# Attention scores turned round: keys on the partitions, the greatest score through two small turnings, sums through a product with ones

## The chip, the cores and the metric

The kernel runs on one NeuronCore of a Trainium2 chip. The core has five engines that run side by side, each working through its own list of instructions in order. TensorE (PE in the profile; its weight loads are listed as PEld) multiplies matrices and writes its results into PSUM, a small memory of eight banks of 512 fp32 columns on each of 128 partitions. VectorE (DVE), ScalarE (ACT) and GpSimd (POOL) work elementwise on SBUF, the main on-chip memory; of the three only DVE and ACT reach PSUM in this kernel. SyncE (SP) issues DMAs. The metric is the device time of one execution in microseconds (us), as the median of several runs.

## What is computed

Four layers, each added to a residual stream x of 16 batches of 100 tokens and 512 channels: cross attention with 16 heads, a mixture of eight experts, cross attention with 8 heads, and an FFN with quantized weights. The change touches the two attentions alone. All is fp32.

```python
q = (query @ Wq + bq).reshape(B, Nq, H, D).transpose(0, 2, 1, 3)
k = (key_value @ Wk + bk).reshape(B, Nkv, H, D).transpose(0, 2, 1, 3)
v = (key_value @ Wv + bv).reshape(B, Nkv, H, D).transpose(0, 2, 1, 3)
attn = jnp.einsum('bhqd,bhkd->bhqk', q, k) * scale
attn = jnp.clip(attn, -CLAMP, CLAMP)
attn = jax.nn.softmax(attn, axis=-1)
...
x = jnp.einsum('bhqk,bhkd->bqhd', attn, v).reshape(B, Nq, Cq)
return x @ Wo + bo
...
x = x + jnp.tanh(g_xattn[0]) * _L0_xattn_ref(_layernorm(x, axis=-1), ctx_768, ...)
x = x + jnp.tanh(g_ffn[0]) * _L0_ffn_ref(_layernorm(x, axis=-1), ...)
x = x + jnp.tanh(g_xattn[1]) * _L1_xattn_ref(_layernorm(x, axis=-1), ctx_768, ...)
x = x + jnp.tanh(g_ffn[1]) * _L1_ffn_ref(_layernorm(x, axis=-1), ...)
```

A batch has 100 queries (T) and 722 keys (S) whose input has 384 channels. In layer 0 a head has D = 32 channels, so G = 4 heads fill a block of 128 partitions; in layer 1 D = 64 and G = 2. The second attention has no clamp and no biases bq, bk, bv.

## The kernel before

**Steps.** `Attention.run` (L500) goes over 64 steps (b, m): 16 batches, and for each the KC = 4 blocks m of 128 channels. One step handles the G heads of its block. For a step the kernel computes scores, takes exp, turns the exps round and multiplies them with the values.

**Scores** (`scores`, L356). The queries of a head, a slice `qT` of D partitions and 100 columns, are the stationary operand; the keys `kT` stream past in two halves of 361 columns (SH). The result `ps_s` has the queries on the partitions and the keys along the columns. The G heads lie on different partitions of the array and write to different banks. DVE copies them out with the sign turned, and the same instruction gives the least of the negated scores in each row (L389 for layer 1, L402 for layer 0): with queries on the partitions the greatest score of a query lies within one row. In layer 0 the two halves are parts 0 and 1, recorded at different places of a step, and L412 joins their extremes. The array `extremes` keeps them for a later test (`unusual`, L1116) of whether the clamp could have mattered.

**Exp** (`softmax`, L417). ACT computes exp for each head with the negated greatest score as the bias of each row, into one of six (layer 1: four) buffers `pr`, and the same instruction adds up the row (`sums`).

**Turning** (`turn`, L430). The product with the values needs the keys on the partitions. So each head's exps are turned on PE in six pieces of up to 128 keys (L444), 24 pieces a step in layer 0 and 12 in layer 1, and ACT and DVE in turns copy the results from PSUM (L457, L459) to `pT`. The reciprocals of the sums, spread over D columns (L439), are turned likewise (L452), one piece a step.

**Weighted sum** (`attend`, L462). For six pieces of keys and G heads, PE multiplies the values (stationary) with `pT` (100 columns) into `ps_pv`. DVE multiplies the result with the turned reciprocal (L475) and writes it to `tT`.

**What fills the steps.** `run` also deals out units of other work: the keys (`keys`, L208) and values (`values`, L230) of the following batches, 14 units a batch, and the units in `extra`: queries (L332), the inputs of queries (L312), output projections (L482), and in layer 0 the routing work of the experts that follow. A step in layer 0 is recorded in this order: part 0 of the next step's scores, weighted sum of the step before, two fifths of the units, turnings of the first pair of heads, a fifth of the units, part 1 of the next scores, turnings of the second pair, the rest of the units, exp of the next step. In layer 1 all scores are computed together and there is one pair.

**What sets the order.** PE runs its instructions in the order in which they are recorded (`manual_schedule(engines={PE})`); for the other engines a scheduler chooses. Buffers come from pools, and an allocation waits until the last use of the buffer that it reuses is over. PSUM's eight banks are split into `ps_s` (two buffers of two banks, for scores) and `ps_m` (four buffers of one bank, for everything else: `ps_k`, `ps_v`, `ps_q`, `ps_t`, `ps_pv`, `ps_y`, `ps_tr`).

Of the kernel before, what the change touches and what calls it, by code (L numbers as in the profile page):

```python
# [8 lines left out]
F32 = mybir.dt.float32  # L9
# [17 lines left out]
SL = S - (NS - 1) * P  # L27
GB = 4
# [113 lines left out]
class Attention:  # L142
# [43 lines left out]
    def first_keys(self):  # L186
# [3 lines left out]
        two = [self.ps_s.tile([P, 2, 512], F32, tag="s", name="ps_k2") for _ in range(2)]  # L190
        banks = [t[:, c, :SH] for t in two for c in range(2)]
# [63 lines left out]
    def open(self, ctx):  # L255
# [3 lines left out]
        self.p3, self.p4 = pool("3", 3), pool("4", 4)  # L259
        self.ps_s, self.ps_m = pool("s", 2, space=PSUM), pool("m", 4, space=PSUM)  # L260
# [3 lines left out]
        for n in ("bq", "bv"):  # L264
# [6 lines left out]
        self.probs = [  # L271
            self.pw.tile([T, NS * P], F32, name=f"pr{i}_{name}") for i in range(6 if self.G == 4 else 4)
        ]
        for t in self.probs:
            nc.gpsimd.memset(t[:, S:], 0.0)
        self.qT, self.nmax, self.sums, self.negated, self.pT = {}, {}, {}, {}, {}
# [79 lines left out]
    def scores(self, b, m, part):  # L356

        nc, D, G = self.net.nc, self.D, self.G
        g, i = divmod(b, GB)
        q = slice(i * T, (i + 1) * T)  # L360
        if m == 0 and part == 0:
            self.nmax[b] = (
                self.p2.tile([T, self.heads], F32, tag="nm", name=f"nm_{self.name}_{b}")
                if self.extremes is None
                else self.extremes[:, b * self.heads : (b + 1) * self.heads]
            )
            self.sums[b] = self.p2.tile(
                [T, self.heads], F32, tag="sums", name=f"sums_{self.name}_{b}"
            )
        if part == 0:  # L370
            self.negated[b, m] = [
                self.p4.tile([T, S], F32, tag="ns", name="ns") for _ in range(G)
            ]
        pss = [self.ps_s.tile([T, 2, 512], F32, tag="s", name="ps_s") for _ in range(2)]

        banks = [(j, part) for j in range(G)] if G == 4 else [(j, c) for j in range(2) for c in range(2)]
        for n in sorted(range(4), key=lambda n: banks[n][1]):
            j, c = banks[n]
            nc.tensor.matmul(  # L379
                pss[n // 2][:, n % 2, :SH],  # L380
                self.qT[g][j * D : (j + 1) * D, m, q],
                self.kT[b, m][j * D : (j + 1) * D, c * SH : (c + 1) * SH],
                start=True,
                stop=True,
            )
        nm = self.nmax[b][:, m * G : (m + 1) * G]
        if G == 2:
            for j in range(2):
                nc.vector.tensor_scalar(  # L389
                    self.negated[b, m][j].rearrange("p (c s) -> p c s", c=2),  # L390
                    pss[j][:, :, :SH],
                    -1.0,
                    BIG,
                    ALU.mult,
                    ALU.min,
                    accum_out=nm[:, j : j + 1],
                )
            return
        if part == 0:
            self.halves = self.p2.tile([T, 2, G], F32, tag="nmh", name="nmh")  # L400
        for j in range(G):
            nc.vector.tensor_scalar(  # L402
                self.negated[b, m][j][:, part * SH : (part + 1) * SH],
                pss[j // 2][:, j % 2, :SH],
                -1.0,
                BIG,
                ALU.mult,
                ALU.min,
                accum_out=self.halves[:, part, j : j + 1],
            )  # L410
        if part == 1:
            nc.vector.tensor_tensor(nm, self.halves[:, 0, :], self.halves[:, 1, :], ALU.min)  # L412

    def prob(self, b, h):
        return self.probs[(b * self.heads + h) % len(self.probs)]

    def softmax(self, b, m):  # L417
        nc, G = self.net.nc, self.G
        for j, ns in enumerate(self.negated.pop((b, m))):
            h = m * G + j  # L420
            nc.scalar.activation(  # L421
                self.prob(b, h)[:, :S],
                ns,
                AF.Exp,
                bias=self.nmax[b][:, h : h + 1],
                scale=-1.0,
                accum_out=self.sums[b][:, h : h + 1],
            )

    def turn(self, b, m, pair):  # L430


        nc, D, G = self.net.nc, self.D, self.G
        last = pair == G // 2 - 1
        t = self.p3.tile([P, 2 * NS + 1, T], F32, tag="pT", name="pT")
        if last:
            rinv = self.p2.tile([T, G, D], F32, tag="rinv", name="rinv")
            sums = self.sums[b][:, m * G : (m + 1) * G]
            nc.vector.reciprocal(rinv, bcast(sums.unsqueeze(2), T, G, D))  # L439
        for q in range(3):  # L440
            ps = self.ps_m.tile([P, 5, T], F32, tag="mm", name="ps_t")
            for i in range(4):
                j, c = divmod(4 * q + i, NS)
                nc.tensor.transpose(  # L444
                    ps[:, i, :],
                    self.prob(b, m * G + 2 * pair + j)[:, c * P : (c + 1) * P],
                    self.net.ident[:T, :T],
                )
            n = 4
            if last and q == 2:  # L450
                n = 5
                nc.tensor.transpose(  # L452
                    ps[:, 4, :], rinv.rearrange("p g d -> p (g d)"), self.net.ident[:T, :T]
                )
            to = t[:, 4 * q : 4 * q + n, :]
            if (m + pair + q) % 2:
                nc.scalar.copy(to, ps[:, :n, :])  # L457
            else:
                nc.vector.tensor_copy(to, ps[:, :n, :])  # L459
        self.pT[b, m, pair] = t  # L460

    def attend(self, b, m):  # L462
        nc, D, G = self.net.nc, self.D, self.G
        ps = self.ps_m.tile([P, T], F32, tag="mm", name="ps_pv")
        for c in range(NS):
            n = P if c < NS - 1 else SL
            for j in range(G):
                nc.tensor.matmul(  # L468
                    ps[j * D : (j + 1) * D, :],
                    self.v[b][:n, c, m * P + j * D : m * P + (j + 1) * D],  # L470
                    self.pT[b, m, j // 2][:n, j % 2 * NS + c, :],
                    start=(c == 0),
                    stop=(c == NS - 1),
                )
        nc.vector.tensor_tensor(  # L475
            self.tT[:, m, b * T : (b + 1) * T],
            ps,
            self.pT[b, m, G // 2 - 1][:, 2 * NS, :],
            ALU.mult,
        )  # L480
# [18 lines left out]

    def run(self, given, after_project=None, more=()):  # L500
# [3 lines left out]
        parts = 2 if self.G == 4 else 1  # L504
# [1096 lines left out]
```

## Time and profile before

Three runs gave 2827.48, 2832.17 and 2833.72 us, a median of 2832.17. The profiled execution took 2827.75 us, its span from first to last instruction 2826.0 us.

| stretch (us from the start) | what runs | length | PE busy | DVE busy | ACT busy | POOL busy |
|---|---|---|---|---|---|---|
| 62 to 936 | layer 0, most of the steps | 874 | 867.8 | 440.8 | 431.2 | 21.9 |
| 936 to 956 | layer 0, its last steps | 20 | 17.4 | 14.5 | 15.2 | 0.8 |
| 1200 to 1640 | experts | 440 | 439.6 | 41.3 | 36.2 | 16.1 |
| 1840 to 2400 | layer 1, most of the steps | 560 | 560.0 | 190.1 | 201.4 | 8.2 |
| 2400 to 2826 | end of layer 1, FFN | 426 | 414.2 | 84.8 | 68.7 | 43.3 |

Views used below. *Sums by stage* give for a stretch its length and the busy time (and count) of PE, PEld, DVE, ACT and POOL, then the clock that PE was granted (1.00 is full), the share of DMA and GB/s. The *timeline* lists instructions in order of time, alike ones that follow each other merged: start, time from the first one's start to the last one's end, engine, line, operation, result and operands, shape, count, and in brackets an idle time before and what ended it. In a matmul's shape 32*100 is the stationary operand (partitions * columns) and 32x361 the streaming one. An ordinary fp32 product appears as two matmul records, a turning as one. Since matmuls overlap, what one costs is the time to the next start, not its own length.

### The profile page before, as it was taken

How to read it: one execution, taken by the hardware profiler on the slowest of the kernel's cores; microseconds unless marked ns; L12 is line 12 of the kernel's file. 1: busy time of each engine (PE TensorE's matmuls, PEld its weight loads, DVE VectorE, ACT ScalarE, POOL GpSimd, SP SyncE). 2: the span in 40 equal slices, each digit the busy share in tenths (PEclk: the TensorE clock that was granted, in tenths of full speed). 3: DMA queues.
4: the chain of work that ended last, by engine and by line, in shares of the span. 5: the costliest groups of instructions: out<-in, count | busy, mean ns of one | idle time of the engine just before them, and what ended most of it. 6: DMA issues, size and time to landing. Idle time of an engine off the chain costs nothing. (4 is left out here: it accounts for less than half of the span.)

```text
span 2826.0 us, 41052 instructions
## 1 busy us (share of the span) xinstructions
PE 2787.1 (99%) x17360; PEld 1732.2 (61%) x17360; DVE 933.4 (33%) x2441; ACT 889.4 (31%) x1740; POOL 166.4 (6%) x187
## 2 busy tenths in 40 slices
PE   8999999999999999999999999999999999899999
PEld 4555555555555588887888755555555555544554
DVE  4544544544455600000000045333233333521100
ACT  2544544454454410000000045333333334311110
POOL 2000000000000000000000032000000000211000
PEclk9999999999999999999999999999999999999999
DMA  4000100000000289999999622000000000430000
GB/s 161 17 17 17 33 24 24 17 28 33 17 24 5 83 328 358 321 319 315 312 319 318 223 83 58 32 16 32 16 17 32 16 27 6 133 105 15 11 12 10
DMA packets 129876, 278.04 MB, mean 98 GB/s; under 512 B 5824, under 2 KB 5840, under 8 KB 129168
## 3 DMA queue, kind: packets, MB, share of 16 engines
q1 hardware_dynamic: 117888, 246.80, 25.5%
q0 software_dynamic: 5088, 16.28, 1.7%
q10 hardware_dynamic: 6704, 12.19, 1.1%
q8 instruction: 141, 2.31, 0.3%
q14 instruction: 55, 0.45, 0.1%
HBM read 260.31 MB, written 14.94 MB: 97 GB/s over the span
## 5 line engine op out<-in xcount | busy, mean ns | idle before, releaser
L239 PE MATMUL ps_v<-wv_a,ctx_a 128*128 128x512 f32 (+1 forms) x1152 | 522.0, 597 | 2.0 <-DVE tT_a L475 1.6
L214 PE MATMUL ps_k<-ctx_a,wk_a 128*128 128x361 f32 x1488 | 488.8, 473 | 0.5 <-ACT kT_a L228 0.3
L855 PE MATMUL ps_h<-xT,w 128*128 128x128 f32 x3712 | 421.1, 276 | 3.7 <-DVEq L1485 3.7
L855 PEld LDWEIGHTS ps_h<-xT,w 128*128 128x128 f32 x3712 | 418.6, 193 | 4.4 <-issue 4.4
L214 PEld LDWEIGHTS ps_k<-ctx_a,wk_a 128*128 128x128 f32 x1488 | 272.3, 190 | 153.1 <-issue 15.4
L239 PEld LDWEIGHTS ps_v<-wv_a,ctx_a 128*128 128x128 f32 (+1 forms) x1152 | 203.4, 184 | 235.7 <-issue 227.2
L402 DVE TENSOR_SCALAR_CACHE_REDUCE ns<-ps_s 100x361 f32<-100x361 f32 x512 | 244.3, 526 | 199.5 <-PE ps_s L379 177.6
L444 PEld LDWEIGHTS ps_t<-ident,pr_a 100*128 100x128 f32 x2304 | 215.5, 142 | 81.0 <-issue 40.2
L421 ACT ACTIVATE pr_a<-ns,extremes 100x722 f32<-100x722 f32 x256 | 227.1, 889 | 67.9 <-DVE extremes L412 67.9
L444 PE MATMUL ps_t<-ident,pr_a 100*128 100x100 f32 x2304 | 238.9, 252 | 4.5 <-DVE tT_a L475 4.2
L459 DVE COPY pT<-ps_t 128x400 f32<-128x400 f32 (+1 forms) x288 | 169.7, 593 | 193.9 <-PE ps_t L444 186.1
L379 PE MATMUL ps_s<-kT_a,qT_a 32*100 32x361 f32 (+1 forms) x1536 | 211.7, 499 | 4.2 <-DVE ns L402 2.1
L246 ACT COPY v_a<-ps_v 128x512 f32<-128x512 f32 x192 | 111.0, 579 | 331.8 <-PE ps_v L239 329.8
L875 PE MATMUL ps_o<-w,midT 128*128 128x512 f32 x464 | 203.9, 592 | 0.0
L457 ACT COPY pT<-ps_t 128x400 f32<-128x400 f32 (+1 forms) x288 | 146.9, 510 | 175.2 <-PE ps_t L444 157.8
L389 DVE TENSOR_SCALAR_CACHE_REDUCE ns<-ps_s 100x722 f32<-100x722 f32 x128 | 111.3, 906 | 269.6 <-PE ps_s L379 269.6
L1081 PE MATMUL ps_z<-ffn_w,y_ffn 128*128 128x512 f32 (+1 forms) x416 | 190.8, 594 | 0.0
L1063 PE MATMUL ps_y<-hT,ffn_w 128*128 128x384 f32 (+2 forms) x512 | 185.4, 507 | 0.0
L439 DVE RECIPROCAL rinv<-sums_a 100x128 f32<-100x128 f32 x128 | 121.7, 951 | 182.6 <-ACT pr_a L421 182.3
L468 PEld LDWEIGHTS ps_pv<-pT,v_a 128*32 128x32 f32 (+3 forms) x4608 | 135.4, 120 | 70.9 <-issue 49.8
L866 DVE TENSOR_TENSOR midT<-silu,ps_h 128x512 f32<-128x512 f32 x58 | 39.9, 688 | 388.8 <-PE ps_h L855 388.8
L468 PE MATMUL ps_pv<-pT,v_a 128*32 128x100 f32 (+3 forms) x4608 | 163.6, 253 | 3.0 <-DVE pT L459 1.9
(160 smaller groups left out, 1816.0 us busy)
## 6 DMA issues: line engine op xcount, KB each, us to landing
w<-in_L_ffn_w SPq DMA_DIRECT2D x116, 1024.0 KB, 6.2
w<-in_L_ffn_wo SPq DMA_DIRECT2D x29, 2048.0 KB, 10.2
ctx_a<-in_ctxT SPq DMA_DIRECT2D x30, 1083.0 KB, 5.2
q<-in_L_ffn_fc_q SPq DMA_DIRECT2D x8, 1024.0 KB, 5.5
ffn_w<-in_L_ffn_fc_scales SPq DMA_DIRECT2D x8, 1024.0 KB, 8.2
rows<-ot ACTq DMA_DIRECT2D x29, 256.0 KB, 7.4
xn_d<-xn_moe ACTq DMA_DIRECT2D x12, 256.0 KB, 2.0
ctx_a<-in_ctxT SPq DMA_DIRECT2D x6, 361.0 KB, 5.5
```

What stands on the lines that cost most here:

```text
L214: nc.tensor.matmul(ps, self.wk[:, k, m * P : (m + 1) * P], self.cxs[b][:, k, c * SH : (c + 1) * SH], start=(k == 0), stop=(k == KK - 1),)
L239: nc.tensor.matmul(ps[:n], self.cxs[b][:, k, c * P : c * P + n], self.wv[:, k, :], start=(k == 0), stop=(k == KK - 1),)
L379: nc.tensor.matmul(pss[n // 2][:, n % 2, :SH], self.qT[g][j * D : (j + 1) * D, m, q], self.kT[b, m][j * D : (j + 1) * D, c * SH : (c + 1) ...
L402: nc.vector.tensor_scalar(self.negated[b, m][j][:, part * SH : (part + 1) * SH], pss[j // 2][:, j % 2, :SH], -1.0, BIG, ALU.mult, ALU.min, ...
L421: nc.scalar.activation(self.prob(b, h)[:, :S], ns, AF.Exp, bias=self.nmax[b][:, h : h + 1], scale=-1.0, accum_out=self.sums[b][:, h : h + 1],)
L444: nc.tensor.transpose(ps[:, i, :], self.prob(b, m * G + 2 * pair + j)[:, c * P : (c + 1) * P], self.net.ident[:T, :T],)
L459: nc.vector.tensor_copy(to, ps[:, :n, :])
L468: nc.tensor.matmul(ps[j * D : (j + 1) * D, :], self.v[b][:n, c, m * P + j * D : m * P + (j + 1) * D], self.pT[b, m, j // 2][:n, j % 2 * NS ...
L855: nc.tensor.matmul(ph[:, f, :], w[:, n, k, f * P : (f + 1) * P], self.xT[j][:, k, :], start=(k == 0), stop=(k == KC - 1),)
L875: nc.tensor.matmul(po, self.midT[j, f // 4][:, f % 4, :], w[:, f, :], start=(f == 0), stop=(f == KF - 1),)
L1063: nc.tensor.matmul(ps[:, :nt], w1[f // nf][:, k, f % nf * P : (f % nf + 1) * P], hT[g][:, k, :nt], start=(k == 0), stop=(k == KC - 1),)
L1081: nc.tensor.matmul(z[j][:n], y[:, j * P : j * P + n], w2[f // nf][:, f % nf, :], start=(f == 0), stop=(f == NF - 1),)
```

## The change

Scores are computed the other way round: a piece of up to 128 keys of a head is the stationary operand and the head's 100 queries stream. So the keys are on the partitions from the start, as the product with the values needs them. A step has six pieces for each head, in two parts of three (NS2); the tile `ps_s` now holds one bank for each head, four banks in layer 0 (one buffer) and two in layer 1 (two buffers).

ACT copies each part from PSUM to SBUF (`raw`, two buffers that steps use in turns; the missing 46 rows of the last piece were filled once with -3e38). DVE forms the maximum over the six pieces with five maxima of 400 columns (layer 1: 200). What is left is a maximum across the partitions: `peaks` turns the G blocks of maxima on PE and reduces them along the columns on DVE (`top`); `softmax` turns `top`, repeated over 128 columns, back on PE, so that each partition has each query's greatest score in `ps_top`. DVE subtracts it from `raw` in two halves of 1200 columns (layer 1: 600), ACT takes exp in place, and POOL adds the six pieces up in five additions (`sm`).

`turn` goes away. `attend` multiplies the values with `pT` as before, and multiplies `sm` with ones, so that each of a head's D output rows holds the sum; DVE takes the reciprocal of that and multiplies.

The order of a step becomes: part 0 of the next scores, units, part 1 of the next scores, weighted sum of the step before, units, peaks, units, softmax of the next step, units. A function `cut` divides the units by their columns into fixed shares. A step -1 is added in front, in which the queries of blocks 1 to 3 are computed. `unusual` tests the greatest scores instead of the least negated ones.

```diff
@@ open_first keys and pools
-        two = [self.ps_s.tile([P, 2, 512], F32, tag="s", name="ps_k2") for _ in range(2)]
-        banks = [t[:, c, :SH] for t in two for c in range(2)]
+        G = self.G
+        two = [self.ps_s.tile([P, G, 512], F32, tag="s", name="ps_k2") for _ in range(4 // G)]
+        banks = [t[:, c, :SH] for t in two for c in range(G)]
...
-        self.p3, self.p4 = pool("3", 3), pool("4", 4)
-        self.ps_s, self.ps_m = pool("s", 2, space=PSUM), pool("m", 4, space=PSUM)
+        self.ps_s, self.ps_m = pool("s", 4 // self.G, space=PSUM), pool("m", 4, space=PSUM)
...
-        self.probs = [
-            self.pw.tile([T, NS * P], F32, name=f"pr{i}_{name}") for i in range(6 if self.G == 4 else 4)
+        self.raw = [
+            self.pw.tile([P, 2, self.G, NS2, T], F32, name=f"raw{i}_{name}") for i in range(2)
         ]
-        for t in self.probs:
-            nc.gpsimd.memset(t[:, S:], 0.0)
+        for t in self.raw:
+            nc.gpsimd.memset(t[:, 1, :, NS2 - 1, :], -BIG)
@@ scores
+        ps = self.ps_s.tile([P, G, 512], F32, tag="s", name="ps_s")
+        for n in range(NS2):
+            c = part * NS2 + n
+            r = P if c < NS - 1 else SL
+            for j in range(G):
+                nc.tensor.matmul(
+                    ps[:r, j, n * T : (n + 1) * T],
+                    self.kT[b, m][j * D : (j + 1) * D, c * P : c * P + r],
+                    self.qT[g][j * D : (j + 1) * D, m, q],
+                    start=True,
+                    stop=True,
+                )
+        st = self.raw[(b * KC + m) % 2]
         if part == 0:
+            self.mx[b, m] = self.p2.tile([P, G, T], F32, tag="mx", name="mx")
+            nc.scalar.copy(st[:, 0].rearrange("p g c t -> p g (c t)"), ps[:, :, : NS2 * T])
+        else:
+            n = NS2 - 1
+            nc.scalar.copy(
+                st[:, 1, :, :n, :].rearrange("p g c t -> p g (c t)"), ps[:, :, : n * T]
+            )
+            nc.scalar.copy(st[:SL, 1, :, n, :], ps[:SL, :, n * T : NS2 * T])
+        mx = self.mx[b, m]
+        for n in range(NS2):
+            if part or n:
+                nc.vector.tensor_tensor(
+                    mx, st[:, part, :, n, :], mx if part or n > 1 else st[:, 0, :, 0, :], ALU.max
+                )
+
+    def peaks(self, b, m):
+        nc, G = self.net.nc, self.G
+        mx = self.mx.pop((b, m))
+        ps = self.ps_m.tile([T, G, P], F32, tag="mm", name="ps_mx")
         for j in range(G):
+            nc.tensor.transpose(ps[:, j, :], mx[:, j, :], self.net.ident)
...
+        nc.vector.tensor_reduce(self.top[b, m], ps, AX.X, ALU.max)
@@ softmax
+        top, st = self.top.pop((b, m)), self.raw[(b * KC + m) % 2]
+        ps = self.ps_m.tile([P, G, T], F32, tag="mm", name="ps_top")
+        for j in range(G):
+            nc.tensor.transpose(ps[:, j, :], bcast(top[:, j : j + 1], T, P), self.net.ident[:T, :T])
+        t = self.p2.tile([P, 2, G, NS2, T], F32, tag="pT", name="pT")
+        sm = self.p2.tile([P, G, T], F32, tag="sm", name="sm")
+        for part in range(2):
+            nc.vector.tensor_tensor(
+                t[:, part], st[:, part], bcast(ps.unsqueeze(2), P, G, NS2, T), ALU.subtract
+            )
+            nc.scalar.activation(t[:, part], t[:, part], AF.Exp)
+            for n in range(NS2):
+                if part or n:
+                    nc.gpsimd.tensor_tensor(
+                        sm, t[:, part, :, n, :], sm if part or n > 1 else t[:, 0, :, 0, :], ALU.add
+                    )
@@ attend, after the products with the values
+        for j in range(G):
+            nc.tensor.matmul(
+                ps[j * D : (j + 1) * D, 1, :],
+                self.net.ones[:, :D],
+                sm[:, j, :],
+                start=True,
+                stop=True,
+            )
+        rs = self.p2.tile([P, T], F32, tag="rs", name="rs")
+        nc.vector.reciprocal(rs, ps[:, 1, :])
+        nc.vector.tensor_tensor(self.tT[:, m, b * T : (b + 1) * T], ps[:, 0, :], rs, ALU.mult)
@@ run
+            shares = (0.27, 0.35, 0.24, 0.14) if self.G == 4 else (0.0, 0.52, 0.28, 0.2)
+            u = self.cut(units, shares)
             if nxt:
                 self.scores(*nxt, 0)
+            do(u[0])
+            if nxt:
+                self.scores(*nxt, 1)
+            if i > 0:
                 self.attend(*steps[i - 1])
...
+            do(u[1])
+            if nxt:
+                self.peaks(*nxt)
+            do(u[2])
             if nxt:
                 self.softmax(*nxt)
+            do(u[3])
```

## The prediction

> **What bounds the kernel now.** I read the page's first table, then its 40 slices, then the sums by stage, then single stretches of TensorE's (PE's) timeline.
>
> ```profile
> PE 2787.1 (99%) x17360; PEld 1732.2 (61%) x17360; DVE 933.4 (33%) x2441; ACT 889.4 (31%) x1740; POOL 166.4 (6%) x187
> 62.00:936.00 874.00, 867.77 (x7038) 505.25 (x7037) 440.80 (x1447) 431.24 (x893) 21.90 (x24) 1.00 0.07 23
> 1840.00:2400.00 560.00, 560.00 (x3098) 318.42 (x3098) 190.08 (x376) 201.40 (x407) 8.15 (x8) 1.00 0.06 21
> ```
>
> The second line is the step loop of layer 0, the third most of layer 1's (length, then busy PE, PEld, DVE, ACT, POOL, clock, DMA share). In both PE has no gaps to speak of, the clock is full, DMA is idle; DVE and ACT are half used and POOL is free. The attention loops are PE's, so a step's price is the sum of its PE pieces. The starts of the weighted sums (ps_pv) lie 14.33 us apart in layer 0 and 12.57 in layer 1, which is a step. The expert and FFN stages are not edited.
>
> The pieces, in start order (start, length, operation, count):
>
> ```profile
> 503.94 0.87 PE L379 MATMUL ps_s<-kT_a,qT_a 32*100 32x361 f32 x8
> 504.74 1.24 PE L468 MATMUL ps_pv<-pT,v_a 128*32 128x100 f32 x48
> 505.91 1.06 PE L638 MATMUL ps_logits<-wg_sb,xnT_moe 128*128 128x8 f32 x8
> 506.82 2.07 PE L214 MATMUL ps_k<-ctx_a,wk_a 128*128 128x361 f32 x6
> 508.73 1.19 PE L444 MATMUL ps_t<-ident,pr_a 100*128 100x100 f32 x12
> 509.76 1.71 PE L214 MATMUL ps_k<-ctx_a,wk_a 128*128 128x361 f32 x5
> ...
> 2001.68 1.47 PE L379 MATMUL ps_s<-kT_a,qT_a 64*100 64x361 f32 x8
> 2003.08 1.25 PE L468 MATMUL ps_pv<-pT,v_a 128*64 128x100 f32 x24
> 2004.26 2.95 PE L339 MATMUL ps_q<-tT_a,wq_a 128*128 128x400 f32 x8
> ```
>
> From start to next start: a half of layer 0's scores 0.80, a weighted sum 1.17, twelve turnings 1.03 (0.086 each). A product has two records (two passes), a turning one: turnings were cheap. Four heads run side by side: 48 passes of ps_pv in 1.17 are 12 rounds of four at 0.098, while a 361-column pass alone costs 2.07/6, some 0.32.
>
> **PE's sum, layer 0, one step.** Before: scores 2 x 0.80, 24 turnings and that of rinv 25 x 0.086 = 2.15, weighted sum 1.17: 4.92. After:
> - Scores: 24 products, 48 passes, 12 rounds of four heads. The stationary side is now 128 key columns instead of 100 query columns, and only 100 columns stream. Which of the two paces a round? The logits row streams 8 columns against 128 stationary ones and takes 0.91/8 = 0.112 a pass: that is the pace of loading, above the 0.098 of ps_pv. With some 0.20 for entering and leaving (0.80 less two streams of 0.30) a half costs 0.20 + 6 x 0.112 = 0.87, both 1.74.
> - Weighted sum 1.17, and two more rounds for the product with ones, 0.20.
> - Peaks: 4 turnings that stream 128 columns, 4 x 0.11 = 0.44. Top: 4 x 0.086 = 0.34.
>
> Together 3.89, **1.03 less**; 64 steps: -66 us. Layer 1: before 1.40 + 1.18 + 13 x 0.086 = 3.70; after 0.20 + 12 x 0.112 = 1.54, 1.38, 0.22 and 0.17: 3.31, **0.39 less**; -25 us. PE alone: -91.
>
> A rule speaks against this: the Trainium skill, "TensorE: Matmul & The Clock Gate", section "LDWEIGHTS", says that loading time goes with the columns and that 32 rows of 128 columns take as long as 128 rows. If 48 loads stood in line, the scores would cost 48 x 0.112 + 0.40 = 5.8 a step. The trace shows the loads of the four heads on top of each other:
>
> ```profile
> 511.69 0.27 PEld L379 LDWEIGHTS ps_s<-kT_a,qT_a 32*100 32x100 f32 x8 [0.51 <-issue]
> ```
>
> Eight loads of about 160 ns each fill 0.27 us. So I take rounds of four, and keep the line for a rival.
>
> **The other engines.** Lengths come from rows of the trace, scaled by columns. ACT copies 400 columns in 0.49 and 500 in 0.575: 1200 in 1.16, 800 in 0.82. Exp took 0.889 for 722: 1200 about 1.2. DVE's rows of 361 and 722 columns follow each other by 0.46 and 0.84: a maximum of 400 takes 0.50, a subtraction of 1200 takes 1.35. Reciprocal 0.95 for 128: 0.80 for 100. The reduction (512) about 0.62. POOL's add of 512 takes 1.27: 1.0 for 400. Per step in layer 0 DVE has 2.5 + 2.7 + 0.8 + 0.6 + 0.25 = 6.9 us against about 6.3 removed (eight reductions, three copies, rinv, product), ACT 4.9 against about 5.7, POOL 5.0 new. None exceeds 14 us, so throughput bounds nothing. Lateness does: PE runs in program order and now waits twice a step, at part 1 of the scores (ps_s is one buffer in layer 0, free when ACT has copied part 0) and at peaks (five maxima). Everything recorded behind these on PE waits too, key and value units included. A maximum that waits holds up on DVE the reciprocal and the product that free ps_pv, one of four ps_m buffers; an exp that waits holds up on ACT the copies of keys and values. Both are freed within a step, and PE asks for a buffer again after four allocations, most of a step: I cost that at nothing. Were it late, PE would lose it before a unit instead of at peaks, not in addition.
>
> **The shared port.** Maxima (DVE) and adds (POOL) both read two SBUF operands. The nearest row is the FFN's DVE gate, with two SBUF inputs beside POOL's adds:
>
> ```profile
> 2427.10 0.75 DVE L1018 SCALAR_TENSOR_TENSOR x<-xn_ffn,tgf,x 128x512 f32<-128x512 f32 x1 [0.51 <-POOL xn_ffn L123]
> 2429.60 1.76 DVE L1018 SCALAR_TENSOR_TENSOR x<-xn_ffn,tgf,x 128x512 f32<-128x512 f32 x1
> 2428.30 5.41 POOL L1027 TENSOR_TENSOR x<-x,ffn_b 128x512 f32<-128x512 f32 x4
> ```
>
> The same instruction takes 0.75, or 1.76 when it comes during a POOL add; four adds take 5.41 where 4 x 1.27 = 5.1. The Trainium skill, "SBUF — State Buffer", section "Who interferes with whom", says why: such a DVE instruction and a POOL instruction that reads SBUF exclude each other for a whole instruction. By it each maximum can wait 1.0 for an add; by the unhindered row 0. I take the lock, in turns.
>
> **Two steps laid out** (us from the end of a top turning, order of the built program).
> *No unit after top, then one key unit (1.88) in each gap.* DVE subtracts to 1.5 and 2.85; ACT: exp to 2.8, copy of part 0 to 4.0, exp to 5.2. PE: scores to 0.87, unit to 2.75, waits for ps_s to 4.1 (**1.35**), part 1 to 5.0, weighted sum 6.35, unit 8.2. Adds 1 and 2 hold the port to 4.9; then in turns maximum 5.4, add 6.4, maximum 6.9, add 7.9, maximum 8.4, add 9.4, maximum 9.9, reciprocal 10.7 (it stands ahead of the last maximum), maximum 11.2. Peaks at 11.3 instead of 8.2: **3.1** lost. Without the lock: 8.5, lost 0.3.
> *A value unit (2.64) after top.* Its copy and both exps stand ahead of ACT's copy of part 0: 5.8. PE wants ps_s at 5.4: 0.5 lost; peaks at 11.3 instead of 10.0: 1.3. Sum 1.8.
>
> In the built order, of the 60 middle steps 29 are of the second kind (1.7 on average), 20 of the first (3.0, since many have a longer unit in front), 11 have a query or output product that covers all. So +109 us in layer 0, +46 without the lock. In layer 1 maxima and adds are half as long, ps_s has two buffers and the gap ahead of peaks holds two units: no loss there. But in every second step nothing stands between peaks and top, and PE waits out the reduction, 0.17 + 0.35 + 0.17 = 0.7: 31 x 0.7 = +22. Last steps, without units to cover: layer 0's last three start 8 apart now, laid out 12: +13; layer 1 +5.
>
> **Clock.** In this trace one gap of 0.86 among turnings brought a half clock:
>
> ```profile
> 867.29 1.05 PE L444 MATMUL ps_t<-ident,pr_a 100*128 100x100 f32 x8 [0.86 <-DVE tT_a L475]
> 867.90:871.30 3.40, 3.40 (x10) 1.97 (x8) 1.06 (x3) 0.49 (x1) 0.00 (x0) 0.50 0.00 0
> ```
>
> Such a stretch costs 1.7 us. Bounds: none, or one in each of the 49 steps that wait (83). Layer 0 has two more gaps of 0.86 (at 458 and 637) that left the clock full; one in three, with gaps up to 3 us to come. I take six, +10.
>
> Loads, SP's queue, the memsets and the two inequalities of the guard change nothing on the path.
>
> **Sum:** -91 + 109 + 22 + 18 + 10 = +68 on the profiled execution's 2827.75 us, so 2896; the median of the runs lies 4 above it, and I say 2898.
>
> **Rivals.**
> - *The lock hardly bites* (POOL ahead of or behind the maxima, or DVE keeps the port between maxima): -91 + 46 + 22 + 8 + 5 = -10, 2820. For: PSUM operands don't lock, POOL has idle time. Against: the 1.76. 0.20; another 0.06 that it lands as no change. That also the waits vanish (2740): 0.06.
> - *Clock halves in most short steps:* +73 more, 2970. For: stalls of 3 us fill a stretch. 0.12.
> - *Loads stand in line:* scores +4.0 and +1.35 a step, +344, less some 60 of stalls that they cover: about 3180. It decides from 0.03 a load on. 0.05.
> - Main case: 0.51.
>
> Slower by over 0.2% (5.7 us, what a measurement can tell) 0.68, within 0.06, faster 0.26. The range leaves out the serial loads above and the vanished waits below: 2795 to 2985; the main case alone spans 2850 to 2945.
>
> **What would show it.** ps_s: starts of a part 0.87 apart. PE's idle at peaks: over 1 us on average in layer 0, released by DVE mx. Maxima of 0.5 beside ones of 1.5. PE below 95% in layer 0. I am wrong if DVE's maxima all last 0.5, or if PE shows no gaps at ps_s and peaks.

## The result, and the profile after

The changed kernel takes 2875.6 us (median of 4 runs, 2872.5 to 2878.6); the kernel before took 2831.3 us beside it. The ratio is 1.0158, with a 95% interval of 1.0139 to 1.0177: slower by 1.6%. The profiled execution took 2872.77 us with a span of 2871.1.

The page's first table and its row of clocks, for the kernel after:

```profile
PE 2712.1 (94%) x19536; PEld 1730.1 (60%) x19536; DVE 1180.5 (41%) x1833; ACT 855.3 (30%) x1324; POOL 740.3 (26%) x821
...
PEclk9999999999999799999999999999999999899999
```

PE's busy time fell by 75 us, yet the span grew by 45: PE now stands still. The sums by stage tell where (length, then busy PE, PEld, DVE, ACT, POOL, clock, DMA share, GB/s):

```profile
62.00:936.00 874.00, 796.19 (x8216) 475.82 (x8217) 575.36 (x696) 391.20 (x516) 372.94 (x324) 0.99 0.06 21
1840.00:2400.00 560.00, 548.08 (x3575) 328.97 (x3574) 253.79 (x488) 199.52 (x381) 143.15 (x228) 1.00 0.07 23
974.00:992.00 18.00, 13.50 (x135) 9.15 (x136) 7.00 (x12) 4.86 (x4) 5.15 (x5) 0.53 0.02 8
```

In layer 0's loop PE is at 91% where it had 99%; in layer 1's it is at 98% where it had 100%. The third line lies behind layer 0's loop, where the clock is half. What PE waits for, from its list of waits (sum in us, times, longest):

```profile
PE ps_mx L399 <- DVE mx L389: 70.4, 50, 4.5
PE ps_s L369 <- ACT raw_a L379: 29.3, 32, 3.1
PE ps_top L413 <- DVE top L405: 20.5, 32, 2.7
...
PE ps_pv L444 <- POOL sm L423: 5.0, 2, 3.2
```

Before the change the rows of the step's own products in this list came to 4.2 us at most (ps_t). One step shows how the largest comes about, PE first (start, length, operation, count, idle time before it):

```profile
517.93 0.87 PE L369 MATMUL ps_s<-qT_a,kT_a 32*128 32x100 f32 x24
518.74 1.24 PE L435 MATMUL ps_pv<-pT,v_a 128*32 128x100 f32 x48
519.79 0.36 PE L444 MATMUL ps_pv<-sm,ones 128*32 128x100 f32 x8
520.08 2.09 PE L216 MATMUL ps_k<-ctx_a,wk_a 128*128 128x361 f32 x6
523.85 0.64 PE L399 MATMUL ps_mx<-ident,mx 128*100 128x128 f32 x4 [1.68 <-DVE mx L389]
```

and the same stretch on DVE, then on POOL:

```profile
518.52 1.30 DVE L389 TENSOR_TENSOR mx<-raw_a,mx 128x400 f32<-128x400 f32 x1
520.18 2.29 DVE L389 TENSOR_TENSOR mx<-raw_a,mx 128x400 f32<-128x400 f32 x2 [0.36 <-ACT raw_a L382]
522.40 0.77 DVE L452 RECIPROCAL rs<-ps_pv 128x100 f32<-128x100 f32 x1
523.09 0.70 DVE L389 TENSOR_TENSOR mx<-raw_a,mx 128x400 f32<-128x400 f32 x1
```

```profile
518.02 5.34 POOL L423 TENSOR_TENSOR sm<-pT,sm 128x400 f32<-128x400 f32 x4
```

Two maxima take 2.29 us while POOL adds from 518.02 to 523.36, and PE's turning of the maxima comes 1.68 us after the key unit is through. Over layer 0's loop the maxima read so (minimum, median, maximum in ns):

```profile
L389 DVE TENSOR_TENSOR mx<-raw_a,mx x220: 503/1028/1523, 107.1 to 899.0; 128x400 f32<-128x400 f32 x110
```

Half a microsecond at best, over one at the median. The adds themselves read 1025/1246/1394 where the same instruction takes 1034 at the median in experiment 7, mostly away from the maxima: both sides are held up. One part of the wait is not POOL's: VectorE's reciprocal (0.77) stands ahead of the last maximum, as experiments 9 and 12 take up.

The lost 45 us, read at landmarks of PE's timeline (start of a weighted sum, or of a stage's first product):

| up to | before | after | shift | added in this stretch |
|---|---|---|---|---|
| layer 0, 2nd weighted sum | 84.9 | 93.9 | +9.0 | +9.0 |
| layer 0, 61st (59 steps) | 930.4 | 954.1 | +23.7 | +14.7 |
| experts, first product | 1011.0 | 1041.8 | +30.8 | +7.1 |
| layer 1, 3rd | 1695.8 | 1741.2 | +45.4 | +14.6 |
| layer 1, 61st (58 steps) | 2425.0 | 2464.4 | +39.4 | -6.0 |
| FFN, first product | 2467.1 | 2512.7 | +45.6 | +6.2 |
| end | 2826.0 | 2871.1 | +45.1 | -0.5 |

A step costs 14.58 us in layer 0 (14.33 before) and 12.47 in layer 1 (12.57). So the two loops together lose 9 us, and the few steps at the starts and ends of the layers lose 36.

### The profile page after: what moved, and what is told of

Its sections match the earlier page's. It is cut to its first block, busy times and chain, and to the rows that moved or that the text cites. A ratio compares the mean times of both kernels' runs of the same rounds, so it can differ in the third digit from the quotient of the medians.

```text
span 2871.1 us, 45678 instructions
## 1 busy us (share of the span) xinstructions
PE 2712.1 (94%) x19536; PEld 1730.1 (60%) x19536; DVE 1180.5 (41%) x1833; ACT 855.3 (30%) x1324; POOL 740.3 (26%) x821
## 3 DMA queue, kind: packets, MB, share of 16 engines
q10 hardware_dynamic: 6704, 12.19, 1.1%
## 5 line engine op out<-in xcount | busy, mean ns | idle before, releaser
L216 PE MATMUL ps_k<-ctx_a,wk_a 128*128 128x361 f32 x1488 | 502.8, 479 | 0.7 <-DVE qT_a L354 0.7
L423 POOL TENSOR_TENSOR sm<-pT,sm 128x400 f32<-128x400 f32 (+1 forms) x512 | 462.7, 904 | 39.2
L389 DVE TENSOR_TENSOR mx<-raw_a,mx 128x400 f32<-128x400 f32 (+1 forms) x512 | 366.1, 715 | 30.5 <-ACT raw_a L382 7.1
L417 DVE TENSOR_TENSOR pT<-raw_a,ps_top 128x1200 f32<-128x1200 f32 (+1 forms) x256 | 268.0, 1088 | 238.7 <-PE ps_top L413 238.6
L423 POOL TENSOR_TENSOR sm<-pT 128x400 f32<-128x400 f32 (+1 forms) x128 | 105.5, 824 | 988.6 <-ACT pT L420 950.8
L420 ACT ACTIVATE pT<-pT 128x1200 f32<-128x1200 f32 (+1 forms) x256 | 238.5, 952 | 152.9 <-DVE pT L417 152.6
L369 PEld LDWEIGHTS ps_s<-qT_a,kT_a 32*128 32x128 f32 (+3 forms) x4608 | 184.4, 183 | 133.4 <-issue 62.5
L369 PE MATMUL ps_s<-qT_a,kT_a 32*128 32x100 f32 (+3 forms) x4608 | 218.8, 281 | 33.7 <-ACT raw_a L379 29.3
L389 DVE TENSOR_TENSOR mx<-raw_a 128x400 f32<-128x400 f32 (+1 forms) x128 | 90.6, 708 | 239.2 <-ACT raw_a L379 239.1
L819 POOL DMA_INDIRECT xt<-xn_d,map_i x29 | 27.6, 952 | 564.0 <-PE ps_xT L832 524.4
```

Of the source, the lines that this page charges most:

```text
L216: nc.tensor.matmul(ps, self.wk[:, k, m * P : (m + 1) * P], self.cxs[b][:, k, c * SH : (c + 1) * SH], start=(k == 0), stop=(k == KK - 1),)
L369: nc.tensor.matmul(ps[:r, j, n * T : (n + 1) * T], self.kT[b, m][j * D : (j + 1) * D, c * P : c * P + r], self.qT[g][j * D : (j + 1) * D, ...
L389: nc.vector.tensor_tensor(mx, st[:, part, :, n, :], mx if part or n > 1 else st[:, 0, :, 0, :], ALU.max)
L417: nc.vector.tensor_tensor(t[:, part], st[:, part], bcast(ps.unsqueeze(2), P, G, NS2, T), ALU.subtract)
L420: nc.scalar.activation(t[:, part], t[:, part], AF.Exp)
L423: nc.gpsimd.tensor_tensor(sm, t[:, part, :, n, :], sm if part or n > 1 else t[:, 0, :, 0, :], ALU.add)
```

## The experiments

My theory: PE's own work became cheaper, and it gives the gain back in waits for one chain per step (copies, maxima, peaks, exp), made long by POOL's adds and VectorE's maxima that can't run at the same time. Rivals: the chain is too long even without the adds; PE gained less than thought; the half clock costs the time.

**1. Leave out most of the adds.**

```diff
-            for n in range(NS2):
-                if part or n:
-                    nc.gpsimd.tensor_tensor(sm, t[:, part, :, n, :], ...)
+        nc.gpsimd.tensor_tensor(sm, t[:, 1, :, NS2 - 1, :], t[:, 0, :, 0, :], ALU.add)
```

> Leaves out four of POOL's five additions a step, so the sums are over two pieces of keys instead of six; everything else of the changed kernel stays. Port theory (a maximum on DVE waits for a whole addition on POOL): the maxima of 400 columns fall from 1.0 us to about 0.5 (nothing holds the port), PE's waits for mx in layer 0 fall from 58 to about 12 us, those for ps_s stay at about 28; the whole takes 2820 to 2835 us, 40 to 55 less than 2873. Chain theory (the waits come from the number of steps between top and peaks, whatever POOL does): maxima stay long, waits and time stay within 10 us of the changed kernel's.

Measured: 2802.1 us, ratio to the kernel before 0.9895 (0.9876 to 0.9915). That is 73 us less, more than either theory gave. The maxima and PE's waits in this kernel:

```profile
L389 DVE TENSOR_TENSOR mx<-raw_a,mx x235: 505/575/1520, 101.4 to 899.2; 128x400 f32<-128x400 f32 x118
```

```profile
PE ps_s L369 <- ACT raw_a L379: 27.6, 29, 3.0
PE ps_mx L399 <- DVE mx L389: 20.9, 17, 2.9
```

The median maximum is 0.575, and in layer 0's loop the waits for mx fell from 53 to 5.8 us; those for ps_s stayed at 23.5. Without the adds the chain behind peaks fits. But work was left out, so this alone doesn't separate the port from the work.

This run also divides the 36 us of the starts and ends. At the same landmarks it adds 5.9 at layer 0's start (90.8 for 84.9), 0.2 at its end, 10.9 at layer 1's start and 4.5 at its end, and takes 0.6 off in the FFN: 21 us. So some 15 us there belong to the adds, and 21 remain with one add left.

**2. Keep all adds, take maxima by an operation with one SBUF input.**

```diff
+        to = mx if part == 0 else self.p2.tile([P, G, T], F32, tag="mx1", ...)
+        nc.vector.tensor_reduce(to, st[:, part].rearrange("p g c t -> p g t c"), AX.X, ALU.max)
+        if part:
+            nc.vector.tensor_tensor(mx, mx, to, ALU.max)
```

It stands in place of the five pairwise maxima.

> Same result by other instructions: three of the maxima of a part become one DVE reduction along the columns, which has one SBUF input, and one maximum joins the two parts. Port theory: a reduction of 1200 columns takes about 1.35 us whether POOL adds or not, DVE's work for the maxima falls from 5 x 1.03 to about 3.2 us a step, PE's waits for mx in layer 0 fall from 58 to about 20 us, the time to 2830 to 2845 us. Chain theory: 2 x 1.35 + 0.5 is more than 5 x 0.5, so the chain gets longer and the time is that of the changed kernel or up to 20 us more.

Measured: 2841.7 us, ratio 1.0040 (1.0027 to 1.0052). VectorE's instructions:

```profile
L388 DVE TENSOR_REDUCE mx<-raw_a x114: 1444/1536/1560, 104.1 to 899.1; 128x400 f32<-128x1200 f32 x114
L390 DVE TENSOR_TENSOR mx<-mx,mx x56: 506/512/1343, 108.9 to 889.1; 128x400 f32<-128x400 f32 x56
```

All 114 reductions take 1.44 to 1.56 us, although the adds run beside them as before: this form isn't held. It agrees with the Trainium skill, "SBUF — State Buffer", section "Who interferes with whom", by which a reduction never contends with GpSimd while an operation with two SBUF inputs does. The waits for mx in layer 0's loop are 28.9 us (53 with pairwise maxima), although two reductions and a maximum (2 x 1.54 + 0.51 = 3.6 us) stand where five unhindered maxima would take 2.9. With experiment 1 this settles that maxima and adds hold each other up, and that the form of the instruction decides whether they do.

**3. PE alone.** Copies, maxima, reductions, subtractions, exps and adds are gone; PE's products read constant tiles.

```diff
-        mx = self.mx.pop((b, m))
+        mx = self.c_mx
...
-        t, sm = self.pT.pop((b, m))
+        t, sm = self.c_t, self.c_sm
```

> Leaves out the copies, maxima, reductions, subtractions, exps and additions of both attentions; peaks, top, the weighted sums and the sums read constant tiles. PE's instructions and their order stay. Port theory and the sum of the prediction: PE's own work is 91 us less than before, so the time is about 2735 us (2720 to 2750), steps of layer 0 start about 13.3 apart and of layer 1 about 12.1. Rival (the new products cost PE as much as the turnings did, and the waits cost little): about 2800 us or more.

Measured: 2690.2 us in one execution, span 2688.5, clock 0.997. PE's new work alone takes 140 us less than the kernel before, part of which was idle time of that kernel. A step takes 12.93 us in layer 0 and 12.04 in layer 1, without idle time:

```profile
507.34 0.88 PE L373 MATMUL ps_s<-qT_a,kT_a 32*128 32x100 f32 x24
508.14 1.24 PE L404 MATMUL ps_pv<-c_t_a,v_a 128*32 128x100 f32 x48
509.20 0.35 PE L413 MATMUL ps_pv<-c_sm_a,ones 128*32 128x100 f32 x8
509.49 2.09 PE L216 MATMUL ps_k<-ctx_a,wk_a 128*128 128x361 f32 x6
511.41 0.60 PE L387 MATMUL ps_mx<-ident,c_mx_a 128*100 128x128 f32 x4
```

That is below my range: the rival that PE gained little falls, PE's part of the change was worth more than I had computed, and 185 us were given back.

**4. Deal the units of layer 0 so that none stands after top.**

```diff
-            shares = (0.27, 0.35, 0.24, 0.14) if self.G == 4 else (0.0, 0.52, 0.28, 0.2)
+            shares = (0.41, 0.35, 0.24, 0.0) if self.G == 4 else (0.0, 0.52, 0.28, 0.2)
```

> Layer 0's filler units are dealt out so that none stands after top: the share of that gap goes to the gap behind part 0 of the scores. ACT's copy of part 0 is then no longer behind two exps and a unit's copy. Own theory (the two waits of a step lie on one chain, copy then maxima then peaks): the ps_s waits of layer 0 fall from 25 us to below 8, but the mx waits grow by nearly as much, since the maxima are held by the adds all the same: within 10 us of the changed kernel's 2875.6, so 2866 to 2886. Rival (waits add up independently): the ps_s waits go and nothing takes their place, about -25, so 2850.

Measured: 2882.9 us (2881.2 to 2884.4), within the range of my theory by its total, but not by its parts:

```profile
PE ps_mx L399 <- DVE mx L389: 62.2, 44, 5.4
PE ps_s L369 <- ACT raw_a L379: 40.8, 27, 3.4
```

The waits for ps_s grew from 29 to 41 us. That no unit stands ahead of the scores on PE doesn't make their copy earlier; experiment 8 shows why.

**5. Units behind peaks in every step of layer 1.**

```diff
+            shares = (0.27, 0.35, 0.24, 0.14) if self.G == 4 else (0.0, 0.38, 0.42, 0.2)
```

> Layer 1's shares (0.0, 0.38, 0.42, 0.2) instead of (0.0, 0.52, 0.28, 0.2): a unit now stands between peaks and top in every step. Own theory: PE's waits for top in layer 1 (31 of about 0.6, 18 us) nearly vanish, and a few for mx come (up to 5 us): 2858 to 2866 us. Rival (the wait moves on to the next place in the chain): the waits for mx grow by as much as those for top fall, and the time stays at 2873 to 2878.

Measured: 2867.8 us (2865.9 to 2872.3), ratio 1.0132. A step of layer 1 fell from 12.47 to 12.34 us and its waits for top (17.5 us in the loop) vanished; 9.3 us of waits for mx came in their place, since the unit was taken from the gap ahead of peaks, and the first steps of layer 1 idled 18 us for 14. It gained 8 us, a little less than I expected.

**6. Keep PE warm at the ends.** Dummy products, which nothing reads, stand in the gaps of the last steps and of layer 1's first.

```diff
+            if nxt and self.G == 4 and i >= 60:
+                self.warm(3)
...
+            if nxt and (i >= 60 or (self.G == 2 and i <= 0)):
+                self.warm(2)
```

> Three dummy products ahead of part 1 of the scores (layer 0's last four steps) and two ahead of peaks (both layers' last steps and layer 1's first) fill PE's waits with work that nothing reads. Clock theory: a part of the lost time at the starts and ends is half clock that the waits bring (17 us of it at 974, three of 6.8 us in layer 1's start); with PE kept busy there these stretches shrink, and the time falls by 5 to 12 us, to 2864 to 2871. Rival (the chain alone sets the ends, the half clock falls in waits anyway): no change or up to 5 us slower, 2875 to 2881.

Measured: 2874.1 us (2872.4 to 2875.3), ratio 1.0150 (1.0136 to 1.0164). The stretch behind layer 0's loop, in the sums by stage:

```profile
974.00:992.00 18.00, 12.02 (x140) 7.47 (x139) 7.67 (x15) 3.69 (x3) 5.15 (x5) 0.73 0.29 106
```

Its clock is 0.73 for 0.53, and the half-clock time of the whole kernel fell from 97 to 73 us, but the time didn't move. The last product with ones of layer 0 waits for POOL's sums in both kernels and starts at 985.0 for 985.3: where PE waits for a chain anyway, a slower PE costs little, and the rival holds. The dummies take PE's time themselves, so this is no price of the half clock alone.

**7. Adds behind the next step's peaks.** All work is done; a one-column copy from the next top holds POOL back.

```diff
+    def total(self, b, m, after):
+        t, sm = self.pT[b, m]
+        if after:
+            nc.gpsimd.tensor_copy(sm[:T, 0, 0:1], self.top[after][:, 0:1])
+        for n in range(1, 2 * NS2):
+            nc.gpsimd.tensor_tensor(sm, t[:, n // NS2, :, n % NS2, :], ...)
...
                 self.peaks(*nxt)
+            if i >= 0:
+                self.total(*steps[i], nxt)
```

> The same work in another order: POOL's five adds of a step are put behind the next step's peaks (a one-column POOL copy from the next top holds them there), so that they no longer run beside the maxima. Port theory: maxima of 400 columns go back to about 0.50, the mx waits of layer 0 fall from 53 us to about 6, as when four adds were left out; the ps_s waits of about 24 stay: 2800 to 2812. Rival (the gain of leaving adds out came from less work, or the adds now come too late for the product with ones): waits appear at ps_pv<-sm instead, and the time stays above 2840.

Measured: 2820.5 us, ratio 0.9967 (0.9954 to 0.9980): the order alone makes the change a small gain over the kernel before. Its maxima and PE's waits:

```profile
L389 DVE TENSOR_TENSOR mx<-raw_a,mx x236: 509/574/1548, 102.5 to 899.9; 128x400 f32<-128x400 f32 x118
```

```profile
PE ps_s L369 <- ACT raw_a L379: 29.6, 33, 3.1
PE ps_mx L399 <- DVE mx L389: 21.2, 17, 2.9
...
PE ps_pv L449 <- POOL sm L429: 15.4, 7, 5.4
```

In layer 0's loop it equals the kernel without the adds (13.65 us a step against 13.67), with 8.1 us of waits for mx: the port, not the adds' work, was the price there, (14.58 - 13.65) x 59 = 55 us. My range was missed by 8 us because of the last row: at the ends of the layers the product with ones now waits for late sums. The rival was right there and nowhere else.

**8. Adds late, and no unit of layer 0 after top.** Experiments 4 and 7 together.

```diff
+            shares = (0.41, 0.35, 0.24, 0.0) if self.G == 4 else (0.0, 0.52, 0.28, 0.2)
```

> Adds behind peaks and, besides, no unit of layer 0 after top, so that the copy of part 0 comes earlier. With the port free, own theory has the ps_s waits of about 24 us go as well and little come in their place: 2780 to 2792. Rival (the mx wait only hides behind the ps_s wait): mx waits of 15 us or more come back, and the time is within 8 us of the kernel with the adds behind peaks alone.

Measured: 2829.4 us (2827.8 to 2830.8), 9 us slower than experiment 7. The waits for ps_s in the loop rose from 25 to 35 us, and those for mx stayed at 7.6: both theories missed. ScalarE shows the cause, in a step that starts with the scores at 531.14:

```profile
532.82 1.21 ACT L420 ACTIVATE pT<-pT 128x1200 f32<-128x1200 f32 x1 [1.33 <-DVE pT L417]
533.93 1.14 ACT L379 COPY raw_a<-ps_s 128x1200 f32<-128x1200 f32 x1
534.97 1.21 ACT L420 ACTIVATE pT<-pT 128x1200 f32<-128x1200 f32 x1
```

By PE's timeline the scores of part 0 are done at 532.07, but ScalarE's list has an exp ahead of their copy, and this exp waits for the subtraction. PE's key unit ends at 534.09, and part 1 of the scores starts at 535.12. A unit after top gives the exp its time; taking it away makes the wait longer.

**9. The copy ahead of both exps** (on top of experiment 7).

```diff
             if nxt:
                 self.scores(*nxt, 0)
+            if i >= 0:
+                self.exps(*steps[i])
```

The two exps are recorded here and no longer in `softmax`, and copy and exps of layer 0 are held in this order.

> Adds behind the next step's peaks, as before, and ScalarE's order changed in layer 0: its copy of part 0 of the next scores comes ahead of the two exps of a step, not between them. Order theory: PE's wait for ps_s (25 us with the adds behind peaks, 35 us when no unit stood after top) is the copy standing behind an exp that itself waits for the subtraction; with the copy first the ps_s waits of layer 0 fall below 5 us and the time to 2793 to 2803. Rival (the exps are then late for the product with the weights, or the wait passes on to peaks): ps_pv or mx waits grow by 15 us or more and the time stays within 6 us of 2820.

Measured: 2815.6 us (2811.4 to 2817.2), ratio 0.9947. PE's waits:

```profile
PE ps_mx L401 <- DVE mx L391: 41.8, 28, 4.4
...
PE ps_s L369 <- ACT raw_a L379: 4.0, 3, 1.3
```

In layer 0's loop the waits for ps_s fell from 25 to 2.7 us, as my theory said, and those for mx rose from 8 to 26, as the rival said; the time fell by 5 us only. Both waits lie on one chain. Removing the first lets part 1 of the scores start early, and the wait reappears at peaks. What it consists of, on VectorE in one such step (PE turns these maxima at 271.43, after 0.83 us idle):

```profile
269.07 1.19 DVE L391 TENSOR_TENSOR mx<-raw_a,mx 128x400 f32<-128x400 f32 x2 [0.49 <-ACT raw_a L384]
270.17 0.78 DVE L466 RECIPROCAL rs<-ps_pv 128x100 f32<-128x100 f32 x1
270.86 0.51 DVE L391 TENSOR_TENSOR mx<-raw_a,mx 128x400 f32<-128x400 f32 x1
```

A reciprocal stands inside the chain, ahead of its last maximum.

**10. Early adds at the ends** (on top of 9).

```diff
-                self.total(*steps[i], nxt)
+                self.total(*steps[i], nxt if 0 < i < 59 else None)
```

> The kernel with the copy first, but in the last five steps and the first of each layer the adds are free to run as soon as their exp is there, since no units cover them. The late adds cost some 15 us in waits of the product with ones at the two ends (ps_pv <- sm): these go, and the maxima of the last steps are held instead by a few us: 8 to 13 us less than the kernel with the copy first. Rival (the ends are set by the chain through peaks, which the early adds lengthen by as much): within 4 us of it.

Measured: 2812.6 us (2810.9 to 2812.8), 3 us less: within the rival's 4. The waits for the sums went from 16 to 6 us (two at layer 0's end), but those for mx at the starts and ends of the layers grew from 16 to 22. The ends have no units to hide either chain.

**11. Layer 1's shares of experiment 5** (on top of 10).

```diff
+            shares = (0.27, 0.35, 0.24, 0.14) if self.G == 4 else (0.0, 0.38, 0.42, 0.2)
```

> As the one with early adds at the ends, and besides layer 1's units dealt out so that one stands behind peaks in every step (as in the run of that alone, which gained 8 us of the changed kernel's time): the top waits of layer 1 of some 15 us go; 6 to 12 us less again, so 2775 to 2790, faster than both kernels. Rival: the units taken from the gap ahead of peaks leave the maxima uncovered, and mx waits of about 9 us take most of it back, 0 to 5 us less.

Measured: 2800.3 us (2798.5 to 2800.8), ratio 0.9896 (0.9880 to 0.9913), 12 us less. The gain is at the upper end of what I expected, but the time misses the range, since experiments 9 and 10 had gained less than expected. A step of layer 1 fell from 12.43 to 12.19 us, more than the 0.13 of experiment 5: 5.9 us of waits for mx came back in its loop, for 9.3 there.

**12. The last maximum ahead of the reciprocal** (on top of 11), by holding these two of layer 0 in the order in which they are recorded.

```diff
+                if part and n == NS2 - 1 and G == 4:
+                    self.net.tc.keep_in_program_order(ins)
...
+        ins = nc.vector.reciprocal(rs, ps[:, 1, :])
+        if G == 4:
+            self.net.tc.keep_in_program_order(ins)
```

> As the kernel with all three, and in layer 0 VectorE's last maximum of a step stands ahead of the reciprocal of the weighted sum (it stood behind it, so that the chain copies, maxima, peaks held 0.78 us of other work). Chain theory: with the port free the mx waits that the earlier copy brought (26 to 30 us in layer 0, 0.85 or 1.7 at a time) are this chain; taking a reciprocal of 0.7 out of it cuts them to 5 to 14 us and the time to 2778 to 2788. Rival (the last copy of ScalarE is what is late, the reciprocal ran in its shadow): the mx waits fall by less than 5 us and the time stays within 5 us of 2800.

Measured: 2790.9 us (2789.0 to 2793.6), ratio to the kernel before 0.9869 (0.9852 to 0.9885). The waits for mx in layer 0's loop fell by 9 us, between the two theories: typical ones went from 0.83 and 0.85 to 0.23 and 0.41. VectorE in the step that matches the one of experiment 9:

```profile
268.89 1.86 DVE L391 TENSOR_TENSOR mx<-raw_a,mx 128x400 f32<-128x400 f32 x3 [0.33 <-ACT raw_a L384]
270.67 0.78 DVE L468 RECIPROCAL rs<-ps_pv 128x100 f32<-128x100 f32 x1
```

In experiment 9 the reciprocal took 0.69 of the chain (270.17 to 270.86). But from the first of these maxima to the end of the last it is now 1.86 us for 2.30, only 0.44 less: maxima that follow each other directly start 0.61 and 0.68 apart, and the reciprocal started 0.49 behind the maximum ahead of it. ScalarE's last copy isn't what limits this step: there it was over at 269.42, before the reciprocal began. This version leaves out nothing that the changed kernel computes; it differs by the order of work, the shares and the one-column copies. It is 1.3% faster than the kernel before and 2.9% faster than the changed one (2790.9 / 2875.6).

## Why the prediction was right, and where its terms were off

2898 was forecast with slower as the likely side; 2875.6 was measured. The mechanism held: PE waits at part 1 of the scores and at peaks, released by ScalarE's copy and VectorE's maxima, and the maxima are held by POOL's adds. Its terms, with the experiment without waits (span 2688.5) as the point between:

| term | predicted | measured | from |
|---|---|---|---|
| PE's own work, loop of layer 0 | -66 (64 steps) | -82.4 (59 steps) | 14.33 to 12.93 a step |
| PE's own work, loop of layer 1 | -25 (64 steps) | -30.8 (58 steps) | 12.57 to 12.04 |
| starts and ends, PE cheaper and idle time of before gone | no term | -24.3 | rest of 137.5 |
| given back, loop of layer 0 | +119 (waits 109, clock 10) | +97.2 | 12.93 to 14.58 |
| given back, loop of layer 1 | +22 | +24.8 | 12.04 to 12.47 |
| given back at starts and ends | +18 | +60.6 | rest of 182.6 |
| sum | +68 | +45.1 | spans |

The two rests are of the differences of the spans, 2826.0 - 2688.5 and 2871.1 - 2688.5. The +18 had been laid out from before to after; on that footing the landmarks give 13.3 for the last steps and 23.6 for the starts.

- **PE's pieces.** The rounds of four heads were right: half of the scores costs 0.83 in the experiment without waits, for 0.87 computed from the pace of loading, and the new pieces together 3.84 for 3.89. The rival in which the loads stand in line is out. Too small was the side of before: its pieces cost 5.15 a step on average (5.06 at the median), not 4.92, since 25 turnings took 2.39 (2.30 at the median) where I had taken 0.086 each from one group of twelve. With the 0.10 a step that PE idled before, 5.15 - 3.84 + 0.10 = 1.41 a step, for 1.40 measured. (Two quotients of the prediction are off: the pass of 361 columns is 1.91/6 from start to start, not 2.07/6, and 0.91/8 is 0.114.)
- **Waits in layer 0.** PE's idle time in the loop is 79 us (53 for mx, 25 for ps_s), for 109. A step that waits was sized well: those with a unit after top are 29, as counted, and lose 1.5 us each, for 1.7; of those without one the waiting steps lose 2.65 each, for 3.0. But only 12 of these 30 wait more than 0.3 us, where I had counted 20: in the others two units or a projection lie in a gap (3.9 to 6.6 us of products) and cover the chain.
- **Without the lock** I had 46 us of waits; with the adds late the loop has 34.
- **The port** was to cost 109 - 46 = 63 us, and costs 55 by the loop of experiment 7. The prediction took from the page that it cites that each instruction excludes the other for its whole length, so that an add and a maximum take 1.5 us. The trace differs, and it decides: an add with one maximum beside it is followed by the next add after 1.33 at the median, and an add without one after 1.12, in layer 0's loop. So they hold each other up, but not for the whole of their recorded lengths.
- **Layer 1.** The top waits of +22 are 17.5 us in 29 waits.
- **Clock.** The six stretches of 3.4 us for which I took +10 came out nearly so: layer 0's loop has half clock at 346.0 and 581.6 (3.4 us each), at 916.1 (6.8) and at 950.2 (3.9 within the loop), 17.5 us in all. PE was busy in 13.3 of them, so by the same reckoning they cost some 7. They lie in the +97.2, of which 79 are idle time. Most of the half clock gathered at the starts and ends, which had no such term: 97 us in the whole kernel, for 42 before. By experiment 6 a quarter of it less changed nothing there.
- **Starts and ends** are the term that failed. The prediction has none for the starts, and "Last steps, without units to cover" stands for 18 us. At layer 0's start one wait alone is 4.45 us, and the second weighted sum is 9.0 us late; layer 1's start gives away 14.6. The last three steps of layer 0 start 8.5 apart, not 12 as laid out; of the 7.1 us lost there 5.3 fall behind the last weighted sum's start, where the product with ones waits 3.23 for the adds. The units that hide the chain in the middle are lacking at both ends of a layer. By experiment 1 the adds make 15 us of these 36; that the other 21 are the rest of the chain is argued from the waits, and no run took it away alone.

That the sum came near the result is luck in part: PE's gain was too small by 47 us and what the starts and ends give back by 43, and these offset each other; the price of waits and clock in layer 0's loop was too large by 22.

## What to carry to other kernels

When work moves off the bounding engine onto others, price the chain of one step against the units that cover it, and the first and last steps on their own, where nothing covers it. Two elementwise engines that both read SBUF are not two engines for free: the same adds, moved behind the maxima, turned a loss of 1.6% into a small gain (0.3%). And after a wait is removed, look for the next one on the same chain before counting the gain; here an earlier copy removed 22 us of waits, and 18 of them came back one step further down the chain.

## What the runs showed of the hardware beyond that

- A VectorE maximum (two SBUF inputs, 400 columns) and a GpSimd add of the same size hold each other up, the shorter one more: the maxima's median went from 0.575 to 1.03 us, the adds' from 1.03 to 1.25. A reduction of 1200 columns beside the same adds kept to 1.44 to 1.56. VectorE's subtraction (one input from SBUF, one from PSUM) took 1.40 at the median both in the changed kernel, where no add runs beside it, and in experiment 7, where the adds do, so moving them there cost VectorE nothing.
- The half clock comes with PE's idle stretches, and what it costs depends on what follows. At the starts and ends, with dummy products in the gaps, it fell by 24 us and the time by 1.5, within the spread. In the loop it is paid: behind an idle 2.88 us a key unit takes 3.34 (at 582.24) where the next one takes 2.01.
- A wait costs PE more than its visible idle time. In the step shown, the key unit takes 2.09 us and then PE idles for 1.68; in the run without waits the product behind such a unit starts 1.92 after it, inside its tail. Over the loop the key units take 4.05 us a step for 3.86 there, 11 us in all, of which some 4.5 are the half clock.
